# Layer 1's sums of a graph attention kernel: two slot tiles as one product of 64 weight columns per head

## The chip, the cores and the metric

The kernel runs on one core of a Trainium2 chip. The metric is the device time of one execution in microseconds (us); a version is stated by the median of its runs. A core has TensorE (PE, matrix products; its loads of weights are listed apart, as PEld), VectorE (DVE), ScalarE (ACT), GpSimd (POOL) and SyncE (SP, which here issues transfers). TensorE multiplies a stationary operand, the weights, of up to 128 rows by 128 columns with a moving operand that streams through, and adds into PSUM. Sixteen DMA engines move data between the memory (HBM) and the core.

## What is computed

Two graph attention layers over 3125 nodes and 53125 edges (each drawn edge in both directions, and a self loop per node), with edges sorted by destination. Cut to what matters here, layer 1 (4 heads of 256 columns, 1024 in all):

```python
xl = (x @ W).reshape(n, heads, out_ch)
e = leaky_relu(alpha_src[src] + alpha_dst[dst], 0.2)
e = exp(e - segment_max(e, dst)[dst])
alpha = e / (segment_sum(e, dst)[dst] + 1e-16)
out = segment_sum(xl[src] * alpha[:, :, None], dst)
```

The last line is the part that the change touches: for each node and head, the weighted sum of the rows `xl[src]` of its edges. A layer norm, a ReLU and a residual product follow, then layer 2 with one head of 768 columns, built in the same way.

## The kernel before

**Node tiles and slot tiles.** Nodes lie in 25 tiles of 128 (the last has 53). The edges of a node tile are laid out by an earlier stage of the kernel in 17 slot tiles of 128 slots each (8 in the last node tile), so that the edges of each quarter (32 nodes) of the tile fall in known slot tiles. `QUARTERS` (L33) says which quarters a slot tile can hold: the fifth, ninth and thirteenth (numbers 4, 8 and 12) lie across two quarters, 0 and 1, 1 and 2, 2 and 3; each other slot tile belongs to one.

```python
QUARTERS = [(0,), (0,), (0,), (0,), (0, 1), (1,), (1,), (1,), (1, 2), (2,), (2,), (2,), (2, 3), (3,), (3,), (3,), (3,)]
ROUNDS = [(0, 5, 9, 13), (1, 6, 10, 14), (4, 11, 15), (2, 8, 16), (3, 7, 12)]
```

**One slot tile's part of the sum.** POOL gathers the 128 source rows of 1024 numbers from `table1` in HBM into a tile `g` (`gather`, L197 and L201; thirteen such tiles are held, so gathers run about three rounds ahead). DVE makes the weights `w` (`weights_of`, L734 and L735): for each slot a one-hot row over the 32 nodes of its quarter, times the slot's attention weight, per head. For a slot tile across two quarters `w` is 64 nodes wide, made in one piece. TensorE then multiplies `w` of a head (32 columns of weights, 128 slots) by `g`'s 256 columns of that head, into the quarter's 32 PSUM partitions of `pa` (L758).

**Rounds.** `ROUNDS` (L34) orders the slot tiles so that each round has four products per head, one for each quarter: in the third round slot tile 4 gives those of quarters 0 and 1, in the fifth slot tile 12 gives those of quarters 2 and 3, and in the fourth slot tile 8 gives those of 1 and 2. The four products of a head stand next to each other in TensorE's order, each with its own quarter of the array's columns. A full round has 16 products of f32, and each f32 product shows in the trace as two weight loads and two matmuls, so 32 records of each. In the last node tile, of 53 nodes, only quarters 0 and 1 exist, and the two halves of a row (heads 0 and 1, heads 2 and 3) lie in different PSUM partitions (0 to 63 and 64 to 127, `half_at`, L188).

**Order of the work.** In `sums` (L655 on) TensorE, ScalarE and VectorE run in the order in which the program is written out. After the products of a round stand the gathers and weights of the next one (`fetch`), and then `step`, which takes one piece of the work beside: the end of an earlier node tile (`finish`, `end1`: own row, norm, transposes at L1174, layer 2's row products at L1196 through `dense`, L182), and pieces of the residual product `later` (L1124, also through L182), as many as `pace` says per round. These products are 128 columns wide; those of the last node tile are 32 and 21 wide (L186). So TensorE's order in this stage is: a round of L758, a stretch of L182 or L1174, a round of L758, and in rounds whose `pace` is zero sometimes two rounds in a row.

Layer 2 has sums of its own (`summed`, L1377, 384 columns wide) with the same rounds; it does not run through `sums`.

Of the kernel before, what the change touches and what calls it, by code (L numbers as in the profile page):

```python
# [32 lines left out]
QUARTERS = [(0,), (0,), (0,), (0,), (0, 1), (1,), (1,), (1,), (1, 2), (2,), (2,), (2,), (2, 3), (3,), (3,), (3,), (3,)]  # L33
# [35 lines left out]
def in_order(  # L69
# [16 lines left out]
    nc = tc.nc  # L86
# [29 lines left out]
    def rows_of(b):  # L116
        return P if b < NB - 1 else LAST
# [4 lines left out]
    def tiles_of(b):  # L122
        return J if b < NB - 1 else JL
# [64 lines left out]
    def half_at(b, i):  # L188

        o = 64 * i if rows_of(b) <= 64 else 0  # L190
        return slice(o, o + rows_of(b))

    def gather(g, table, b, j, whole):

        c = slice(b * J + j, b * J + j + 1)
        if whole:
            nc.gpsimd.indirect_dma_start(  # L197
                out=g, out_offset=None, in_=table[:, :],
                in_offset=bass.IndirectOffsetOnAxis(ap=idx_s[:, c], axis=0))
        else:  # L200
            nc.gpsimd.indirect_dma_start(  # L201
                out=g, out_offset=None, in_=table[:, :],
                in_offset=bass.IndirectOffsetOnAxis(ap=idx_k[:, c], axis=0),
                bounds_check=N - 1, oob_is_err=False)
# [6 lines left out]
    def load_rows(q, t, src_, b):  # L211

        for o, e in pieces(b):
            q.dma_start(t[o:e], src_[b * P + o:b * P + e, :])
# [440 lines left out]
    def sums(heads, cols, table, al, alo_d, ahead, lag, gp, ap, pp, end, more, pace, first=None, delay=0.0):  # L655

        width = heads * cols  # L660
        f = width // 2
        n = min(cols, f)
        running = []
        due = delay

        def step(k):
            nonlocal due
            next(first or iter(()), None)
            for g in list(running):
                if next(g, running) is running:  # L670
                    running.remove(g)
            due += pace[k]
            while due >= 1.0:
                due -= 1.0
                next(more, None)

        def finish(b, own, pa):
            for _ in range(lag):
                yield

            r = rows_of(b)
            v = gp.tile([P, 2, heads], F32, name="aw", bufs=3)[:r]
            aw, share = v[:, 0], v[:, 1]
            ao = asked.pop(b)[:r]
            nc.vector.tensor_scalar(aw, ao[:, :heads, b], has[:r, 1, b:b + 1], has[:r, 2, b:b + 1],
                                    op0=OP.mult, op1=OP.max)
            nc.vector.scalar_tensor_tensor(share, ao[:, heads:, b], has[:r, 0, b:b + 1], aw, op0=OP.mult, op1=OP.add)
            nc.vector.tensor_scalar(share, share, 1e-16, None, op0=OP.add)
            nc.vector.reciprocal(share, share)
            z = gp.tile([P, width], F32, name="z", bufs=2)[:r]  # L690
            for o in range(0, width, n):
                nc.vector.scalar_tensor_tensor(z[:, o:o + n], own[:r, o:o + n], aw[:r, o // cols:o // cols + 1],
                                               pa[half_at(b, o // f), o // f, o % f:o % f + n],
                                               op0=OP.mult, op1=OP.add)
            yield from end(b, z, share)

        asked = {}

        def ask(b):
            ao = asked[b] = ap.tile([128, 2 * heads, NB], F32, name="ao", bufs=3)  # L700
            nc.gpsimd.indirect_dma_start(
                out=ao.rearrange("p v b -> p (v b)"), out_offset=None, in_=alo_d[:, :],
                in_offset=bass.IndirectOffsetOnAxis(ap=at_last[:, b:b + 1], axis=0))

        turns = count()
        owns = {}

        def fetch(b, k):

            got = {}  # L710
            for j in ROUNDS[k]:
                if j >= tiles_of(b):
                    continue
                turn = next(turns)
                g = gp.tile([128, width], F32, name=f"g{turn % ahead}", bufs=1)
                gather(g, table, b, j, turn < ahead)
                got[j] = g, weights_of(b, j)
                place = PLACE[j]
                if place == 4:
                    own = owns[b] = ap.tile([128, width], F32, name="own", bufs=3)  # L720
                    load_rows(nc.sync, own, table, b)
                if b == 1 and place == 11:
                    ask(0)
                if b and place == (13 if tiles_of(b) == J else 5):
                    ask(b)
            return got

        def weights_of(b, j):

            c = b * J + j  # L730
            lo, hi = 32 * QUARTERS[j][0], 32 * QUARTERS[j][-1] + 32
            w = ap.tile([128, heads, hi - lo], F32, name=f"w{hi - lo}", bufs=9 if hi - lo == 32 else 3)
            oh = ap.tile([128, 68], F32, name="oh", bufs=4)[:, :hi - lo]
            nc.vector.tensor_scalar(oh, iota_f[:, lo:hi], rel_s[:, c:c + 1], None, op0=OP.is_equal)  # L734
            nc.vector.tensor_tensor(w, oh[:, None, :].to_broadcast([128, heads, hi - lo]),  # L735
                                    al[:, POS[j], :, b:b + 1].to_broadcast([128, heads, hi - lo]), OP.mult)
            return w

        with tc.manual_schedule(engines={PE, ACT, DVE}):
            ready = fetch(0, 0)  # L740
            for b in range(NB):
                pa = pp.tile([P, 2, 512], F32, name="pa", bufs=2)
                opened = set()
                last_q = (rows_of(b) - 1) // 32
                for k, js in enumerate(ROUNDS):
                    made = []
                    for j, (g, w) in ready.items():
                        for i, q in enumerate(QUARTERS[j]):
                            if q <= last_q:
                                made.append((q, w[:, :, 32 * i:32 * i + 32], g))  # L750
                    order = list(range(0, width, n))
                    if rows_of(b) <= 64:
                        order = [o + i * f for o in range(0, f, n) for i in range(2)]
                    for o in order:
                        for q, w, g in made:
                            to = (o // f, q)
                            p0 = 32 * q + half_at(b, o // f).start
                            nc.tensor.matmul(pa[p0:p0 + 32, o // f, o % f:o % f + n], w[:, o // cols, :],  # L758
                                             g[:, o:o + n], start=to not in opened, stop=False,
                                             skip_group_check=True)  # L760
                            opened.add(to)
                    if k + 1 < len(ROUNDS):
                        ready = fetch(b, k + 1)
                    elif b + 1 < NB:
                        ready = fetch(b + 1, 0)
                    step(k)
                running.append(finish(b, owns.pop(b), pa))
            k = 0
            while running:
                step(k)  # L770
                k = (k + 1) % len(ROUNDS)


    with tc.tile_pool(name="m1", bufs=1) as mp:
# [8 lines left out]
        with tc.tile_pool(name="h0", bufs=1) as hp, tc.tile_pool(name="pm1", bufs=1, space=PSUM) as pm1, \  # L783
# [238 lines left out]
            with tc.tile_pool(name="pq1", bufs=1, space=PSUM) as pp:  # L1022
                with tc.tile_pool(name="sb1", bufs=1) as sb:
                    n = J * H * NB
# [73 lines left out]
        with tc.tile_pool(name="w2", bufs=1, reuse_waits="tile") as wp, tc.tile_pool(name="e1", bufs=2, reuse_waits="tile") as ep, \  # L1098
                tc.tile_pool(name="a1", bufs=1, reuse_waits="tile") as ap, \
                tc.tile_pool(name="g1", bufs=1, reuse_waits="tile") as gp, tc.tile_pool(name="pg1", bufs=1, space=PSUM) as pp:  # L1100
            loaded, made, whole, gone = {}, {}, set(), set()
# [50 lines left out]
            def end1(b, z, share):  # L1152
# [52 lines left out]
                store_rows(nc.sync, table2, b, row)  # L1205

            sums(H, C1, table1, al1, alo1_d, 13, 3, gp, ap, pp, end1, more, (2.5, 3.8, 0, 0, 0.9), first(), -6.3)


    with tc.tile_pool(name="m2", bufs=1, reuse_waits="tile") as mp, \  # L1210
# [3 lines left out]
        f = C2 // 2  # L1214
# [192 lines left out]
        with tc.manual_schedule(engines={PE, ACT, DVE}):  # L1407
# [6 lines left out]
            made = softmax(0)  # L1414
# [9 lines left out]
            for b in range(NB):  # L1424
                pa = pp.tile([P, 2, 512], F32, name="pa")
                opened = set()
                for k in range(len(ROUNDS)):
# [3 lines left out]
                    if b + 1 < NB:  # L1431
                        if k < 3:
                            values(b + 1, k + 2)
                        if k == 2:
                            made = softmax(b + 1)
# [489 lines left out]
```

## Time and profile before

| | |
|---|---|
| median of 3 runs | 1917.48 us (1916.97 to 1924.33) |
| the profiled execution's own time | 1923.87 us |
| its span (first to last instruction) | 1922.0 us |
| mean granted TensorE clock | 0.96 |
| layer 1's sums, by L758's first and last start | 507.0 to 1228.2 us |
| L758: matmul records, median duration of one | 3912, 379 ns |
| L758: weight loads, median duration of one | 3912, 110 ns |

The profile is of one execution, so its times are added up against its own 1923.87 us, of which 1922.0 us lie between the first and the last instruction. A matmul's duration contains the way through the array; matmuls overlap, so durations of records may not be added. "Busy" counts overlapping records once. In a row of a group stand the line, the engine, the operation, what is written and read, the weights' rows and columns (128\*32 is 128 rows by 32 columns) and the moving operand's, the count, then the busy time and the mean duration of one, then the engine's idle time before such instructions and what ended it. "issue" is idle time that ended with no releaser that the profile shows. The granted clock is the share of its full clock that TensorE got.

### The profile page before, as it was taken

The numbers are of one execution on the slowest core, as the hardware profiler recorded it, in microseconds if no ns is written. First come the engines' busy times: TensorE is split into PE (matmuls) and PEld (weight loads), VectorE is DVE, ScalarE is ACT, GpSimd is POOL, SyncE is SP. The second block draws the span as 40 slices with busy tenths as digits, with TensorE's granted clock in tenths as the row PEclk, the third lists the DMA queues.
The fourth block names the chain that finished last, engine by engine and source line by source line (L and its number), as shares of the span: only waits on it lengthen the run. The fifth ranks groups of instructions, "written<-read, shape, count | busy, mean of one in ns | idle before, by whom it ended". The sixth has DMA issues, their size and how long they took to land. (4 is left out here: it accounts for less than half of the span.)

```text
span 1922.0 us, 31113 instructions
## 1 busy us (share of the span) xinstructions
PE 1759.3 (92%) x11411; PEld 957.8 (50%) x11411; DVE 1000.4 (52%) x2641; ACT 443.7 (23%) x1286; POOL 898.9 (47%) x922
## 2 busy tenths in 40 slices
PE   8999998999879999999998998969888898988895
PEld 5666664666446655555554554434333333333331
DVE  7673434888845566466466556312433443344345
ACT  2122331000211212112111211212322332333233
POOL 2000102000365666566566666156566666666662
PEclk9999999999889999999998999889889999989998
DMA  7824538331598999999899999488888998988984
GB/s 236 281 96 144 135 110 295 115 126 64 203 407 314 367 372 348 356 374 385 329 356 378 349 377 333 156 324 313 302 286 324 329 328 325 327 311 310 328 284 157
DMA packets 173673, 540.78 MB, mean 281 GB/s; under 512 B 33086, under 2 KB 58452, under 8 KB 173384
## 3 DMA queue, kind: packets, MB, share of 16 engines
q0 software_dynamic: 100912, 381.05, 55.2%
q1 hardware_dynamic: 68206, 147.26, 21.9%
q10 hardware_dynamic: 4394, 10.39, 1.4%
q8 instruction: 93, 1.52, 0.3%
q14 instruction: 68, 0.56, 0.1%
HBM read 498.62 MB, written 65.62 MB: 294 GB/s over the span
## 5 line engine op out<-in xcount | busy, mean ns | idle before, releaser
L197 POOL DMA_INDIRECT g<-table,idx_s x406 | 405.2, 998 | 411.7 <-DVE m L635 179.2
L201 POOL DMA_INDIRECT g<-table,hi_s x426 | 437.7, 1027 | 291.7 <-issue 88.8
L758 PE MATMUL pa<-g,w 128*32 128x256 f32 x3912 | 275.9, 395 | 32.6 <-issue 23.9
L1377 PE MATMUL pa<-g,w 128*32 128x384 f32 x1956 | 248.8, 510 | 58.9 <-issue 54.4
L182 PE MATMUL pr<-wr,h 128*128 128x384 f32 x768 | 288.0, 516 | 3.8 <-issue 3.8
L182 PE MATMUL p<-w,h1T 128*128 128x384 f32 (+1 forms) x768 | 278.7, 511 | 2.2 <-DVE h1T L1181 1.6
L758 PEld LDWEIGHTS pa<-g,w 128*32 128x32 f32 x3912 | 131.7, 112 | 166.3 <-issue 78.7
L182 PEld LDWEIGHTS pr<-wr,h 128*128 128x128 f32 x768 | 144.8, 200 | 126.2 <-issue 58.2
L182 PEld LDWEIGHTS p<-w,h1T 128*128 128x128 f32 x768 | 145.1, 197 | 123.9 <-issue 32.5
L735 DVE TENSOR_TENSOR w<-oh,al 128x128 f32<-128x128 f32 (+1 forms) x416 | 132.0, 317 | 130.5 <-PE pa L758 75.0
L1377 PEld LDWEIGHTS pa<-g,w 128*32 128x32 f32 x1956 | 63.7, 111 | 221.4 <-issue 208.4
L1341 DVE CUSTOM_DVE_ANT_0 e<-mix,pen 128x640 f32<-128x640 f32 x25 | 20.6, 825 | 290.4 <-remote 132.3
L863 PE MATMUL pm<-w,h0l 128*128 128x344 f32 (+1 forms) x468 | 140.8, 455 | 0.0
L182 PE MATMUL pr<-h0k,wr 128*128 128x256 f32 (+1 forms) x576 | 140.1, 390 | 0.0
L1000 PE MATMUL pm<-h0g,wr 128*128 128x512 f32 x288 | 132.7, 607 | 0.1
L863 PE MATMUL pm<-w,h0g 128*128 128x344 f32 x432 | 131.0, 459 | 0.3 <-ACT h0g L842 0.3
L182 PEld LDWEIGHTS pr<-h0k,wr 128*128 128x128 f32 x576 | 106.2, 190 | 29.5 <-issue 9.0
L931 POOL DMA_DIRECT2D hot_d<-ohd x25 | 13.4, 538 | 219.5 <-DVE own L513 120.6
L734 DVE TENSOR_SCALAR oh<-iota_f,rel_s 128x32 f32<-128x32 f32 (+1 forms) x416 | 113.4, 272 | 0.1
L863 PEld LDWEIGHTS pm<-w,h0l 128*128 128x128 f32 (+1 forms) x468 | 84.8, 185 | 44.1 <-issue 5.7
L863 PEld LDWEIGHTS pm<-w,h0g 128*128 128x128 f32 x432 | 81.9, 193 | 40.8 <-issue 1.7
L1320 ACT ACTIVATE slots<-g 128x32 f32<-128x32 f32 x416 | 65.1, 219 | 117.8 <-DMA g<-table,idx_s 77.7
(288 smaller groups left out, 1666.8 us busy)
## 6 DMA issues: line engine op xcount, KB each, us to landing
s<-slo_d SPq DMA_DIRECT2D x25, 544.0 KB
table<-row SPq DMA_DIRECT2D x24, 512.0 KB
own<-table SPq DMA_DIRECT2D x24, 512.0 KB
h1T_d<-h1T SPq DMA_DIRECT2D x24, 512.0 KB
h<-h1T_d SPq DMA_DIRECT2D x22, 512.0 KB
table<-row SPq DMA_DIRECT2D x24, 392.0 KB
ring<-in_x_dram SPq DMA_DIRECT2D x24, 384.0 KB
xr<-in_x_dram SPq DMA_DIRECT2D x24, 384.0 KB
```

Source lines behind the costliest of these rows:

```text
L182: nc.tensor.matmul(out_, lhsT, rhs, start=start, stop=stop)
L197: nc.gpsimd.indirect_dma_start(out=g, out_offset=None, in_=table[:, :], in_offset=bass.IndirectOffsetOnAxis(ap=idx_s[:, c], axis=0))
L201: nc.gpsimd.indirect_dma_start(out=g, out_offset=None, in_=table[:, :], in_offset=bass.IndirectOffsetOnAxis(ap=idx_k[:, c], axis=0), bound ...
L734: nc.vector.tensor_scalar(oh, iota_f[:, lo:hi], rel_s[:, c:c + 1], None, op0=OP.is_equal)
L735: nc.vector.tensor_tensor(w, oh[:, None, :].to_broadcast([128, heads, hi - lo]), al[:, POS[j], :, b:b + 1].to_broadcast([128, heads, hi - ...
L758: nc.tensor.matmul(pa[p0:p0 + 32, o // f, o % f:o % f + n], w[:, o // cols, :], g[:, o:o + n], start=to not in opened, stop=False, skip_gr ...
L863: nc.tensor.matmul(pm[:r, :C], h0[b][:, k, :], w1[:, k, i * C:(i + 1) * C], start=(k == 0), stop=(k == NK1 - 1))
L931: nc.gpsimd.dma_start(hot_d[b], ohs[b])
L1000: nc.tensor.matmul(pm, wr1[:, k, m * 128:(m + 1) * 128], groups[gi][:, k, :], start=(k == 0), stop=(k == NK1 - 1))
L1320: nc.scalar.activation(slots[b % 2][:, POS[j], :], gs[b, j][:, C2:C2 + 1].to_broadcast([128, 32]), AF.Copy)
L1341: nc.vector.tensor_tensor_reduce(out=e, in0=mix[:, :WIN], in1=pen, scale=1.0, scalar=-BIG, op0=OP.add, op1=OP.max, accum_out=top)
L1377: nc.tensor.matmul(pa[p0:p0 + 32, i, :f], w_, g[:, i * f:(i + 1) * f], start=(i, q) not in opened, stop=False, skip_group_check=True)
```

## The change

For a slot tile whose first quarter is even (slot tiles 4 and 12, and the slot tiles of quarters 0 and 2 alone), the quarters are taken together: one product per head with all of `w`'s columns, 32 for one quarter and 64 for two, written to 32 or 64 partitions of `pa`. Where the first quarter is odd (slot tile 8, across quarters 1 and 2, and those of quarters 1 and 3) the products stay one per quarter. `last_q` still leaves out quarters that the last node tile does not have.

```diff
                     for j, (g, w) in ready.items():
-                        for i, q in enumerate(QUARTERS[j]):
-                            if q <= last_q:
-                                made.append((q, w[:, :, 32 * i:32 * i + 32], g))
+                        qs = [q for q in QUARTERS[j] if q <= last_q]
+                        if qs[0] % 2:
+                            made += [(q, w[:, :, 32 * i:32 * i + 32], g) for i, q in enumerate(qs)]
+                        else:
+                            made.append((qs[0], w[:, :, :32 * len(qs)], g))
...
-                            nc.tensor.matmul(pa[p0:p0 + 32, o // f, o % f:o % f + n], w[:, o // cols, :],
+                            nc.tensor.matmul(pa[p0:p0 + w.shape[2], o // f, o % f:o % f + n], w[:, o // cols, :],
                                              g[:, o:o + n], start=to not in opened, stop=False,
                                              skip_group_check=True)
```

The third round of a node tile (slot tiles 4, 11, 15) then has three products per head, of 64, 32 and 32 columns in this order; the fifth (3, 7, 12) has three of 32, 32 and 64. The other rounds are as before. The gathers, the weights on DVE and the order of all else stay.

## The prediction

> **What bounds the kernel now.** First the page's busy shares and its costliest groups.
>
> ```profile
> span 1922.0 us, 31113 instructions
> PE 1759.3 (92%) x11411; PEld 957.8 (50%) x11411; DVE 1000.4 (52%) x2641; ACT 443.7 (23%) x1286; POOL 898.9 (47%) x922
> ...
> L758 PE MATMUL pa<-g,w 128*32 128x256 f32 x3912 | 275.9, 395 | 32.6 <-issue 23.9
> ```
>
> TensorE is busy 92% of the span, and the products that the change touches (L758, layer 1's sums) are 275.9 us of it. The reader is to see that 3912 records of 395 ns would be 1545 us one after another, so more than five lie over each other at a time: a product's mean duration, or an average per record, is no price here.
>
> The chain that ended last cannot be used for this stage, for its listing in order of time begins behind the stage, in this row:
>
> ```profile
> 1248.95 6.14 PE p L186 x45
> ```
>
> So I go to the table by stages (us of the stretch; busy time and count of PE, PEld, DVE, ACT, POOL; granted clock; DMA share; GB/s). L758 runs from 507 to 1228 us.
>
> ```profile
> 507.00:700.00 193.00, 176.68 (x1422) 106.73 (x1422) 100.04 (x328) 34.85 (x94) 116.93 (x113) 0.95 0.96 362
> 700.00:900.00 200.00, 197.45 (x1598) 116.14 (x1594) 115.62 (x388) 39.06 (x112) 127.24 (x127) 0.99 0.98 367
> 900.00:1100.00 200.00, 190.76 (x1493) 107.81 (x1491) 115.55 (x383) 33.25 (x94) 124.36 (x124) 0.96 0.96 361
> 1100.00:1228.00 128.00, 122.11 (x926) 66.46 (x927) 71.89 (x234) 23.44 (x69) 71.65 (x76) 0.96 0.88 322
> 507.00:1228.00 721.00, 687.00 (x5430) 397.15 (x5433) 403.10 (x1331) 130.60 (x367) 440.18 (x438) 0.96 0.95 356
> ```
>
> TensorE is busy 687 of 721 us in this stage; DVE and POOL have some 300 us to spare. DMA is close behind, at 0.95. So time added on TensorE moves the end, up to the 34 us in which it now waits; time taken off it would soon meet the transfers.
>
> How four quarters lie beside each other is seen in the timeline of TensorE near the end of the stage (start us, duration us, what, count).
>
> ```profile
> 1209.67 1.93 PE L758 MATMUL pa<-g,w 128*32 128x256 f32 x32
> 1211.53 2.86 PE L182 MATMUL p<-w,h1T 128*128 128x384 f32 x8
> 1214.32 1.07 PE L758 MATMUL pa<-g,w 128*32 128x256 f32 x16
> 1215.32 1.09 PE L1174 MATMUL p<-ident,z 128*128 128x128 f32 x8
> ...
> 1222.45 1.06 PE L758 MATMUL pa<-g,w 128*32 128x256 f32 x8
> 1223.44 4.16 PE L182 MATMUL p<-w,h1T 128*128 128x384 f32 x12
> ```
>
> Each f32 product is two records. A full round (four quarters, four heads, two records: 32) holds TensorE from 1209.67 to 1211.53, 1.86 us. Sixteen records hold it 1.00 us, and the eight of the last node tile's round with one slot tile also hold it 0.99 us. Those eight use only two quarters' columns (the two halves of the row lie in different ones), so both bursts are four steps deep. **The price goes by depth, not by records**: (1.86 - 1.00) / 4 steps gives 0.215 us for one step, in which up to four quarters run side by side, and 1.86 - 8 x 0.215 leaves 0.14 us for going into 32 columns and out again; from the 0.99 it is 0.13.
>
> **The change part by part.** *Fewer products.* In each of 24 node tiles the fifth and the thirteenth slot tile drop from two products to one per head: 24 x 2 x 4 products, and 4 more in the last node tile for its fifth, 196 in all, so 392 matmul records and 392 weight loads go. Of the 3912 records 3128 stay 32 columns wide and 392 become 64 wide. By depth this takes nothing off: in the round of slot tiles 4, 11 and 15, quarters 0 and 1 were already side by side with 2 and 3, two steps per head, and the wide product still needs its two steps. Bounds of this part: zero, and by the average per record 392 x 275.9 / 3912 = 27.6 us gained. I take zero, because the eight-record row is the nearest and lies on it.
>
> *Two widths in one round.* Now the round issues, per head, one 64-column product and two 32-column ones (the wide one first in the round of 4, 11, 15, last in that of 3, 7, 12), so the width changes twice per head. No row of before shows a change between 64 and 32. The nearest are the changes between 128 and smaller, and one stretch 53 columns wide:
>
> ```profile
> 291.94 0.38 PE L545 MATMUL pd<-tabd,ohd 128*128 128x96 bf16 x5
> 292.25 10.61 PE L863 MATMUL pm<-w,h0l 128*53 128x344 f32 x36
> 302.80 0.39 PE L545 MATMUL pd<-tabd,ohd 128*128 128x96 bf16 x5
> ...
> 809.62 1.02 PE L182 MATMUL pr<-h0k,wr 128*128 128x256 f32 x4
> 810.58 1.93 PE L758 MATMUL pa<-g,w 128*32 128x256 f32 x32
> ```
>
> Four 256-column steps at full width take 4 x 0.215 = 0.86 us but hold TensorE 0.96 before 32 columns begin: 0.10 us is lost at the change of width alone, though nothing is waited for. The 53-column stretch holds 10.55 us for 36 steps of 344 columns; a step is 344/256 x 0.215 = 0.289, so 0.15 us goes for its change in and out, as much as for 32 columns. [...]
>
> [...]
>
> If the widths take turns, each head has two segments instead of one: two steps for the wide product, then two for the pair. One segment costs 2 x 0.215 + 0.13 = 0.56 us. A round has 4 heads x 2 = 8 segments, 4.48 us, where it took 1.86: **2.62 us more**. There are 24 x 2 = 48 such rounds (the last node tile's fifth slot tile stands alone in its round, on both halves of the row, so it costs one more change, 0.13 us): 48 x 2.62 = **126 us** on TensorE. Bounds: nothing, if the wide product runs beside the two narrow ones; 83 us, if they take turns but nothing is lost at a change (8 x 0.43 + 0.14 - 1.86 = 1.72 per round); 130 us with 0.15 in place of 0.13 for the wide segments. I take 126, since each change of width in the trace has that loss.
>
> *What gives some back.* TensorE waits 34 us in this stage. The waits view of the stage (who waits for whom: us in total, times, longest), with DVE's wait for TensorE in it:
>
> ```profile
> DVE w L735 <- PE pa L758: 75.0, 32, 6.0
> ...
> PE pa L758 <- issue: 23.9, 37, 1.3
> ...
> PE pa L758 <- DMA g<-table,hi_s: 2.9, 3, 2.1
> ```
>
> A place where such waits lie, in the timeline, and the page's group of the gathers:
>
> ```profile
> 932.70 0.39 PE L758 MATMUL pa<-g,w 128*32 128x256 f32 x1 [0.85 <-issue]
> 934.11 0.42 PE L758 MATMUL pa<-g,w 128*32 128x256 f32 x2 [1.02 <-issue]
> 935.56 1.98 PE L758 MATMUL pa<-g,w 128*32 128x256 f32 x15 [1.02 <-issue]
> ```
> ```profile
> L201 POOL DMA_INDIRECT g<-table,hi_s x426 | 437.7, 1027 | 291.7 <-issue 88.8
> ```
>
> Single products here start 1.41 and 1.45 us apart. A gather keeps POOL about 1 us (1027 ns), so I read these as rounds that stand for gathered rows arriving one by one; the view itself says only that it sees no releaser. Such idling also lowers the granted clock, 0.96 against 0.99 in the stretch from 700 to 900 where little is waited for. With 5.2 us more on TensorE per node tile, the gathers come early instead. From 700 to 1228, 528 - 510.3 = 17.7 us are idle, and the clock shortfall is 0.01 x 200 + 0.04 x 200 + 0.04 x 128 = 15 us: at most 33 can come back, at least nothing. I take 20, most of it, because these short waits end once the rows are ahead; the first 193 us, before the gathers have any lead, I leave as they are. Would emptier columns lower the clock? No:
>
> ```profile
> 292.20:302.80 10.60, 10.60 (x40) 4.53 (x37) 2.00 (x12) 2.08 (x6) 0.53 (x1) 1.00 0.62 204
> ```
>
> 53 busy columns for ten microseconds kept it at 1.00.
>
> *Nothing else moves.* Gathers, weights on DVE and stores are issued in the same order; the wide weights are already made in one piece. DVE already waits 75 us for TensorE to free weight buffers and will wait longer, which costs nothing while DVE is not the bound. Layer 2 has its own products and keeps its time.
>
> **Sum.** 126 - 20 = 106 us. The profiled execution took 1923.9 us (1922.0 us of span and 1.9 around it) and would become 2030; it lies 6.4 above the median of the three runs, 1917.5, which becomes **2023 us**.
>
> **The rivals.** *The wide product runs beside the narrow ones* (chance 0.12). Quarters 0 and 1 belong to one and 2 and 3 to the others throughout the round, so no column changes its owner, whereas every change seen in the trace takes over columns of the product before. Against it: the loss was alike for 32 and 53 columns. Then a round stays two steps per head and the time stays at about 1917 us, no change.
>
> *They take turns but lose nothing in between* (0.07). The loss at a change may come from columns that change hands, and a queue that is one for each width would still separate them. 83 - 15 given back = 68 us: 1986 us.
>
> *Records have a price* (0.03). This one ends faster: 27.6 us less, 1890 us, if the average per record held; it decides from the point where fewer records let the four quarters start closer together. Against it stands the row of eight records, which took as long as sixteen, and a DMA share of 0.95 that would not let the stage shrink as far. [...]
>
> **How the numbers follow.** The forecast, turns with a loss at each change, gets 0.78; the rivals 0.12, 0.07 and 0.03. Its own spread goes from 126 - 43 (the 33 given back, and 10 of the 16 us that the first 193 stand idle) to 130 and some more for longer weight loads ahead of 64 columns: 2000 to 2060. The range must leave out no more than 0.2; without the no-change and the faster rival 0.15 is gone, so it reaches down to the second rival with some room, 1975, and up to 2060. About 0.5%, 9.6 us, is what a measurement of this kernel can tell from no change. Slower 0.78 + 0.07 = 0.85, same 0.12, faster 0.03.
>
> **What would show it.** In the profile of the changed kernel L758 should stand in two forms, 392 records 128*64 and 3128 of 128*32, with some 400 us of busy time together. In the timeline, rounds of 24 records should hold TensorE near 4.5 us and pure rounds of 32 still 1.86; the stage should end near 1335 instead of 1228, with its DMA share down to about 0.83 and fewer waits of L758. If rounds of 24 hold 1.86 us, the first rival is right; at 3.6 the second. It would be wrong in size if the waits of L758 stay at 34 us, or if the clock falls in the mixed rounds.

## The result and the profile after

The changed kernel took 2015.8 us (median of 4 runs, 2013.15 to 2029.32) against 1917.2 us (median of 4) before. The ratio is 1.0517 with a 95% interval of 1.0478 to 1.0555: 98.6 us slower. A later measurement, against its own runs of the kernel before, gave 1.0547 (1.0503 to 1.0591). The forecast was 2023 us. The profiled execution took 2013.15 us.

The page of the changed kernel: span, busy shares, the group of the changed products (now L760), and the queue that will matter below.

```profile
span 2011.2 us, 30329 instructions
PE 1847.1 (92%) x11019; PEld 957.5 (48%) x11019; DVE 998.3 (50%) x2641; ACT 445.9 (22%) x1286; POOL 904.9 (45%) x922
...
q8 instruction: 90, 1.47, 0.3%
...
L760 PE MATMUL pa<-g,w 128*32 128x256 f32 (+1 forms) x3520 | 384.3, 392 | 20.9 <-issue 12.7
```

392 records are gone, and the products' busy time has gone up from 275.9 to 384.3 us all the same. The groups of L760 with its two shapes apart (in the stretch from 500 to 1330 us):

```profile
L760 PE MATMUL pa<-g,w 128*32 128x256 f32 x3128 | 282.2, 390 | 20.6 <-issue 12.5 <-DVE w L735 4.7 <-DMA g<-table,hi_s 3.3
...
L760 PE MATMUL pa<-g,w 128*64 128x256 f32 x392 | 125.8, 406 | 0.4 <-issue 0.2 <-DMA g<-table,hi_s 0.2
```

In the tile view of `pa`, L760 starts at 508.7 and last at 1319.1 us: the stage lasts 810 us instead of 721. What lies ahead of it (507.0 and 508.7 us) and behind its last start (693.8 and 692.1 us, the span less that start) kept its length. All of the loss is in this stage, and there it is in the mixed rounds:

```profile
902.57 4.60 PE L760 MATMUL pa<-g,w 128*32 128x256 f32 x24
907.10 2.86 PE L182 MATMUL p<-w,h1T 128*128 128x384 f32 x8
909.79 1.02 PE L182 MATMUL pr<-h0k,wr 128*128 128x256 f32 x4
910.75 1.93 PE L760 MATMUL pa<-g,w 128*32 128x256 f32 x32
912.61 1.09 PE L1176 MATMUL p<-ident,z 128*128 128x128 f32 x8
```

A mixed round of 24 records holds TensorE from 902.57 to 907.10, 4.53 us; the pure round of 32 records behind it still holds it 1.86 us. The forecast had 4.48 and 1.86. The reader should look at starts of neighbours here, not at the durations: the pure round's row lasts 1.93 us, as its last record of 0.38 us runs on into the next line's first. (A merged row prints the shape of its first record; this one, of the fifth round, begins with 32 columns.)

The stage as a whole, in the columns of the table by stages shown before:

```profile
509.00:1319.00 810.00, 789.88 (x5038) 402.25 (x5040) 402.05 (x1330) 130.48 (x367) 439.67 (x438) 0.99 0.88 317
```

TensorE is now idle 20 us in it instead of 34, at a granted clock of 0.99 instead of 0.96, and the DMA share went from 0.95 to 0.88. So TensorE, busy 790 of 810 us, bounds the stage.

### The profile page after: what moved, and what is told of

Same layout as the page of the kernel before. It is cut to its first block, busy times and chain, and to the rows that moved or that the text cites. A ratio compares the mean times of both kernels' runs of the same rounds, so it can differ in the third digit from the quotient of the medians.

```text
span 2011.2 us, 30329 instructions
## 1 busy us (share of the span) xinstructions
PE 1847.1 (92%) x11019; PEld 957.5 (48%) x11019; DVE 998.3 (50%) x2641; ACT 445.9 (22%) x1286; POOL 904.9 (45%) x922
## 3 DMA queue, kind: packets, MB, share of 16 engines
q8 instruction: 90, 1.47, 0.3%
## 5 line engine op out<-in xcount | busy, mean ns | idle before, releaser
L197 POOL DMA_INDIRECT g<-table,idx_s x406 | 414.6, 1021 | 424.1 <-DVE m L635 179.4
L760 PE MATMUL pa<-g,w 128*32 128x256 f32 (+1 forms) x3520 | 384.3, 392 | 20.9 <-issue 12.7
L1379 PE MATMUL pa<-g,w 128*32 128x384 f32 x1956 | 237.9, 513 | 69.7 <-issue 41.0
L182 PE MATMUL p<-w,h1T 128*128 128x384 f32 (+1 forms) x768 | 273.5, 504 | 1.7 <-DVE h1T L1183 1.6
L760 PEld LDWEIGHTS pa<-g,w 128*32 128x32 f32 (+1 forms) x3520 | 139.3, 113 | 257.4 <-issue 185.4
L1379 PEld LDWEIGHTS pa<-g,w 128*32 128x32 f32 x1956 | 61.8, 111 | 224.3 <-issue 176.2
```

The costliest lines, as they stand in the source:

```text
L182: nc.tensor.matmul(out_, lhsT, rhs, start=start, stop=stop)
L197: nc.gpsimd.indirect_dma_start(out=g, out_offset=None, in_=table[:, :], in_offset=bass.IndirectOffsetOnAxis(ap=idx_s[:, c], axis=0))
L760: nc.tensor.matmul(pa[p0:p0 + w.shape[2], o // f, o % f:o % f + n], w[:, o // cols, :], g[:, o:o + n], start=to not in opened, stop=False, ...
L1379: nc.tensor.matmul(pa[p0:p0 + 32, i, :f], w_, g[:, i * f:(i + 1) * f], start=(i, q) not in opened, stop=False, skip_group_check=True)
```

## The experiments

The first three runs share a chip on which the kernel before takes 1804.7 us; the next four share a second chip (1924.65 us), the last three a third (1921.5 us). Only ratios, and differences within a chip, can be compared with the rest.

**Fewer changes of width in a mixed round.** The first run issues the wide products of all four heads, then the narrow ones (two segments a round); the second does so for heads in pairs (four segments). The changed kernel has eight.

```diff
-                    for o in order:
-                        for q, w, g in made:
+                    widths = sorted({w.shape[2] for _, w, _ in made}, reverse=True)
+                    for o, (q, w, g) in [(o, m) for n_ in widths for o in order for m in made if m[1].shape[2] == n_]:
...
+                    for o, (q, w, g) in [(o, m) for os in (order[:2], order[2:]) for n_ in widths for o in os
+                                         for m in made if m[1].shape[2] == n_]:
```

> The changed kernel with another order inside the two mixed rounds of a node tile: first the 64-column products of all four heads, then the 32-column ones, so that the width changes once in a round instead of seven times. Theory (the two widths take turns, and each change of width loses 0.13 us): a mixed round goes from 4.5 us to 16 x 0.215 + 2 x 0.13 = 3.70 us, which is 48 x 0.83 = 40 us less on TensorE; with what is given back, about 1980 us. Rival (the wide product is itself slow, whatever stands beside it): no difference from the changed kernel, 2016 us, the round at 4.5 us. Rival (only the change costs, the widths could share a step): the round falls to about 2.0 us and the time to 1920.

> As the run before, but the heads in two pairs, so the width changes three times in a mixed round. Theory: 16 x 0.215 + 4 x 0.13 = 3.96 us for a round, halfway in the count of changes, about 1992 us. Rival (the wide product is itself slow): 2016 us. If the loss at a change were not a constant, the round would not lie on the line through 4.5 us (eight segments) and the run before (two).

Measured: 1878.4 us, 1.0415 (1.0392 to 1.0438), with two segments, and 1890.0 us, 1.0472 (1.0448 to 1.0495), with four. TensorE's timeline, first with two segments:

```profile
630.16 3.79 PE L761 MATMUL pa<-g,w 128*64 128x256 f32 x24
633.88 2.86 PE L182 MATMUL p<-w,h1T 128*128 128x384 f32 x8
```

and with four:

```profile
633.08 4.06 PE L762 MATMUL pa<-g,w 128*64 128x256 f32 x24
637.07 2.86 PE L182 MATMUL p<-w,h1T 128*128 128x384 f32 x8
```

The rounds hold TensorE 3.72 and 3.99 us. With 4.53 for eight segments the three lie on a line: 0.27 / 2 and 0.54 / 4 are both 0.135 us for a segment, and what is left at none is 3.45 us, sixteen steps of 0.216. Both halves of the theory are seen apart: the widths take turns (3.45 us, where four narrow quarters need eight steps, 1.73), and each segment loses 0.135 us. The rival that only changes cost (2.0 us a round) and the one of a slow wide product (4.5 us whatever the order) both fall. The times were 73.7 and 85.3 us over before, where 63 and 75 had been expected: the rounds were right, what came back was less, 16 and 17 of 89 and 102 us. In the three traces from this chip these products have no wait at all without a named releaser, where the kernel before had 23.9 us of them in its trace from another chip; it was not traced on this one.

**One of the two places.**

```diff
-                        if qs[0] % 2:
+                        if qs[0] % 2 or j == 12:
```

> The changed kernel with the fifth slot tile alone as a wide product; the thirteenth is two 32-column products again. Theory: 24 mixed rounds instead of 48, 63 us more on TensorE than before; with 20 to 30 given back about 1955 us. Rival (the cost is in one of the two places, the wide product first or last in the round): 1917 or 2016 us.

Measured: 1855.5 us, 1.0291 (1.0266 to 1.0316), 50.8 us over its 1804.7. Each place carries its part; a round with the wide product first holds TensorE as long as one with it last (4.53 us in the rows below; the last-placed one of the changed kernel, shown above, 4.53). Of 24 x 2.67 = 64 us added, 13 came back; some 25 had been expected to.

```profile
645.35 4.60 PE L760 MATMUL pa<-g,w 128*64 128x256 f32 x24
649.88 0.59 PE L182 MATMUL p<-w,h1T 128*128 128x384 f32 x1
```

**Wide products without mixing.** Slot tiles 4 and 12 together fill all four quarters, so they can make a round of their own, two wide products side by side. The regrouped rounds are run with narrow products and with the change.

```diff
+ROUNDS1 = [(0, 5, 9, 13), (1, 6, 10, 14), (4, 12), (2, 8, 15), (3, 7, 11, 16)]
...
-                for k, js in enumerate(ROUNDS):
+                for k, js in enumerate(ROUNDS1):
```

> The kernel before, with layer 1's rounds regrouped so that slot tiles 4 and 12 stand alone in the third round (its four quarters come from two slot tiles), then 2, 8, 15 and 3, 7, 11, 16. All products stay 32 columns wide, and every round still has four products per head, each on its own quarter. Both theories: the time of before within 1% (1900 to 1935 us), as no step is added; only the moments at which gathered rows are wanted move.

> The same regrouped rounds with the change: the third round now holds two 64-column products per head, one on quarters 0 and 1 and one on 2 and 3, and no 32-column product; no round is mixed. The same 392 records fewer as in the changed kernel. Theory (the two widths cannot share a step; the wide product alone costs nothing): the third round stays at 8 steps, about 1.9 us with 16 records, and the time equals that of the regrouped kernel with narrow products within 0.5%. Rival (the wide product is itself slow): 24 rounds cost more, some 1960 us. [...]

Measured against before at 1924.65 us: narrow 1933.5 us, 1.0039 (1.0012 to 1.0066); wide 1917.4 us, 0.9978 (0.9953 to 1.0003). The timeline of the wide one:

```profile
625.11 1.95 PE L761 MATMUL pa<-g,w 128*64 128x256 f32 x16
626.99 4.15 PE L183 MATMUL p<-w,h1T 128*128 128x384 f32 x12
631.07 1.93 PE L761 MATMUL pa<-g,w 128*32 128x256 f32 x32
632.93 4.15 PE L183 MATMUL p<-w,h1T 128*128 128x384 f32 x12
```

Sixteen records of 64 columns hold TensorE 1.88 us, the pure narrow round 1.86. So a wide product costs nothing as such; mixing does (4.53 us). Yet the wide one is about 16 us faster by the medians than the narrow one, more than the 0.5% expected, with rounds that take the same time undisturbed. Waits without a named releaser at these products are 22.6 us in the narrow one's trace and 16.2 in the wide one's. This difference, and the one between what was added and what was measured above, needed another cause than changes of width.

**The same TensorE time without a change of width.** Products with zero weights (the tile `zeros`) behind the third and fifth round, on the kernel before, here with six per quarter; the other run has `range(2)`:

```diff
+                    if k in (2, 4) and b < NB - 1:
+                        for _ in range(6):
+                            for q, w, g in made:
+                                nc.tensor.matmul(pa[32 * q:32 * q + 32, 1, f - n:f], zeros, g[:, width - n:],
+                                                 start=False, stop=False, skip_group_check=True)
```

> The kernel before, with two more 32-column products per quarter, of weights that are zero, behind the third and the fifth round of each of the first 24 node tiles: four more steps of 0.215 us, 0.86 us a round, 41 us of TensorE in all, with no change of width. It adds zeros to the sums, so nothing of the computation changes. Theory (the give-back comes first: waits and clock return up to some 30 us, and only what is beyond them shows): about 1930 us. Rival (a fixed share of what is added returns, a quarter): 1949 us.

> The same with six more products per quarter: twelve steps, 2.58 us a round, 124 us of TensorE in all, as much as the change was reckoned to add, again with no change of width. Theory (the time of the changed kernel is nothing but TensorE time added in these rounds, less what the waits and the clock return): within 1% of the changed kernel, 2000 to 2030 us, with the granted clock in the stage near 0.99. Rival (the changes of width do something more, such as keeping weights from being loaded ahead of the next stretch): clearly less than the changed kernel.

Measured: 1966.9 us, 1.022 (1.0166 to 1.0274) with two products, and 2065.5 us, 1.0754 (1.0701 to 1.0808) with six. Both expectations missed, and on the same side: 42 us (by the interval 32 to 53) for 41 added, 141 us (135 to 156) for some 125 added. By the medians nothing came back, and with six, more was lost. An undisturbed round with six:

```profile
647.98 1.93 PE L760 MATMUL pa<-g,w 128*32 128x256 f32 x32
649.73 2.77 PE L767 MATMUL pa<-g,zeros 128*32 128x256 f32 x48
652.44 2.86 PE L184 MATMUL p<-w,h1T 128*128 128x384 f32 x8
```

takes 4.46 us, 2.60 more than a pure one, as reckoned. A disturbed one shows the rest, in TensorE's timeline and in that of its weight loads:

```profile
1020.76 1.96 PE L760 MATMUL pa<-g,w 128*32 128x256 f32 x28
1023.04 0.38 PE L760 MATMUL pa<-g,w 128*32 128x256 f32 x1 [0.32 <-issue]
1023.76 0.39 PE L760 MATMUL pa<-g,w 128*32 128x256 f32 x1 [0.34 <-issue]
1024.48 0.38 PE L760 MATMUL pa<-g,w 128*32 128x256 f32 x1 [0.32 <-issue]
1025.20 0.40 PE L760 MATMUL pa<-g,w 128*32 128x256 f32 x1 [0.35 <-issue]
1025.90 0.53 PE L767 MATMUL pa<-g,zeros 128*32 128x256 f32 x1 [0.30 <-issue]
```
```profile
1023.75 0.13 PEld L760 LDWEIGHTS pa<-g,w 128*32 128x32 f32 x2 [1.29 <-issue]
1025.19 0.11 PEld L760 LDWEIGHTS pa<-g,w 128*32 128x32 f32 x1 [1.32 <-issue]
1025.21 0.11 PEld L767 LDWEIGHTS pa<-g,zeros 128*32 128x32 f32 x1
```

Late gathers can't do this. 28 of the round's 32 records are through, and the zero products read rows that the round has read before them. Single records start 0.72 us apart, loads of weights 1.44 us apart, and the view names nothing that is waited for. The trace of the kernel before had the same, in the row just ahead of the three that the prediction showed:

```profile
930.41 1.45 PE L758 MATMUL pa<-g,w 128*32 128x256 f32 x14
```

A round goes head by head. The first head's 8 records, which ran in two steps of four quarters here too (four starts from 930.41 to 930.43 us, four from 930.65 to 930.67), already read from every gathered tile and every tile of weights of the round. When the single records began, 14 were through, so the rows had arrived.

This looks like instructions that come too slowly. The page counts them in its DMA queues (packets, MB, share), the kernel before first and then the one with six narrow zero products:

```profile
q8 instruction: 93, 1.52, 0.3%
```
```profile
q8 instruction: 111, 1.82, 0.3%
```

0.30 MB for 4608 more records of matmuls and weight loads is 65 bytes a record, so this queue carries TensorE's instructions. The changed kernel, with 784 records fewer of both kinds together, has 90 packets and 1.47 MB. But the queue's packets do not fall where TensorE stands. Around the rows above, the kept trace has one from 1015.29 to 1016.25 us and the next from 1031.33 to 1032.45, none between. Of the 54 waits without a releaser in this stage (25.8 us), 3 overlap a packet, for 0.7 us together, while a packet was under way 7% of the time. So in nearly all of them TensorE was not waiting for a packet of this queue to land; if instructions came slowly, it was somewhere behind the queue.

Two more kernels put the theory to the test: the same streaming, in fewer records. One has three products per quarter of 512 moving columns; the other three of 128 weight columns for all quarters together.

```diff
+                        for _ in range(3):
+                            for q, w, g in made:
+                                nc.tensor.matmul(pa[32 * q:32 * q + 32, 1, :], zeros, g[:, f:],
...
+                        for q, w, g in made[-3:]:
+                            nc.tensor.matmul(pa[:, 1, :], zeros, g[:, f:],
...
```

> The changed kernel once more, on the chip of the two runs that follow. All theories: 1.05 times the kernel before, as in its first measurement.

> The kernel before with zero products behind the third and fifth rounds again, the same 2.56 us of streaming a round as with six narrow products, but three per quarter of 512 moving columns, so 24 records a round in place of 48. It adds zeros to the sums. Theory A (TensorE stands idle in these rounds because its instructions come too slowly: single records start 0.7 us apart in the middle of a round whose operands are all there): fewer records, less standing; between the two, about 1.06 to 1.07 times before. Theory B (it stands for gathered rows): the same TensorE time is added, so 1.075 as with 48 records.

> The same streaming time again, 2.56 us a round, as three zero products of 128 weight columns and 512 moving columns: 6 records a round in place of 48, and no further change of width where a 128-column stretch follows. It adds zeros to the sums. Theory A (instructions come too slowly): TensorE gets 123 us more work and 20 to 35 us of standing come back, as in the changed kernel, so 1.045 to 1.055 times before, with TensorE idle in the stage below 25 us and half the short stalls gone. Theory B (gathered rows): the same 1.075 as with 48 records, as the transfers get as much more time either way.

Measured against before at 1921.5 us: the changed kernel 2032.0 us, 1.0547 (1.0503 to 1.0591); 24 records 2045.9 us, 1.0669 (1.061 to 1.0728); 6 records 2007.9 us, 1.0447 (1.0413 to 1.0481). An undisturbed round with 24 records, then one with 6:

```profile
644.96 1.93 PE L760 MATMUL pa<-g,w 128*32 128x256 f32 x32
646.72 2.76 PE L767 MATMUL pa<-g,zeros 128*32 128x512 f32 x24
649.40 2.86 PE L184 MATMUL p<-w,h1T 128*128 128x384 f32 x8
```
```profile
657.10 1.93 PE L760 MATMUL pa<-g,w 128*32 128x256 f32 x32
658.97 2.84 PE L766 MATMUL pa<-g,zeros 128*128 128x512 f32 x6
661.64 3.72 PE L184 MATMUL p<-w,h1T 128*128 128x384 f32 x11
```

They hold TensorE 4.44 and 4.54 us. Side by side:

| zero products' records in a round | added on TensorE, 48 rounds | measured over before | chip |
|---|---|---|---|
| 48 | 48 x 2.60 = 125 us | 141 us | second |
| 24 | 48 x 2.58 = 124 us | 124 us | third |
| 6 | 48 x 2.68 = 129 us | 86 us | third |

On one chip the same streaming costs 124 or 86 us, by how it is cut up. The transfers got as much more time in all three, so lateness of the gathers (1.075 for all) falls. The step from 48 to 24 records is not shown: it goes from one chip to another, and the intervals of the two ratios overlap. The step from 24 to 6 is clear of noise, but these products differ also in width and in how many run side by side. So it is shown that the same streaming costs 38 us more as 24 records of 32 columns than as 6 of 128; that the number of records is the cause, or the fetching of instructions behind it, is argued, and no run separates it. With 6 records the waits view of the stage and its row by stages read:

```profile
PE pa L760 <- issue: 8.5, 15, 1.1
...
PE pa L766 <- issue: 0.8, 1, 0.8
```
```profile
507.00:1306.00 799.00, 782.71 (x5723) 437.00 (x5722) 403.29 (x1330) 130.24 (x367) 439.69 (x438) 0.99 0.88 321
```

These products' standing without a named releaser went from 23.9 us before to 9.3, idle time from 34 to 16, and the clock from 0.96 to 0.99, as in the changed kernel. With 48 records "issue" stood at 25.8 us (17.8 at the zero products, 8.0 at the others), with 24 at 13.8, and where single records stand a lone record's 0.38 us, counted as busy, covers half of each gap.

## Why the prediction was right, and where it was not

**What bounds the stage** held: time put on TensorE moved the end of the stage (810 us instead of 721 in the changed kernel), and there what lies outside the stage kept its length.

**Price by depth, not by records** held for the array's own time: 392 fewer records took nothing off a round (1.88 us for 16 wide, 1.86 for 32 narrow). It did not hold for the stage as a whole: zero products cut into 24 narrow records a round cost 38 us more than in 6 wide ones, and the regrouped kernel with 392 records fewer was 16 us faster than its narrow twin. That is the direction of the rival in which records have a price, but not its mechanism, four quarters that start closer together: the undisturbed rounds took the same time. Whether the records or something else about narrow products has that second price is not shown.

**Two widths in one round** held in both parts. The segment was put at 0.56 us, from two steps and the loss at changes between 128 and smaller widths; measured, 4.53 / 8 = 0.566. That 64 and 32 columns take turns was the author's estimate, as no row of before has the two side by side; the runs showed it, with 3.45 us left of a mixed round when its segments' losses are taken off, against 1.73 for eight shared steps. Changes between 64 and 32 columns cost what those between 128 and smaller did: 0.135 us a segment against 0.13 to 0.15 a stretch. The rivals in which the widths share a step, or take turns without loss, would have given 1.86 and 3.6 us a round. The pair of wide products in one round ran side by side (1.88 us for 16 records); the mixed ones did not (4.53 us for 24), though they shared no column. 48 x 2.67 = 128 us were added, against 126 forecast.

**What gives some back** is the step that failed, in its reason. The prediction read the short waits as rounds that "stand for gathered rows arriving one by one", because single products stood 1.4 us apart and a gather keeps POOL about 1 us (1027 ns). That was a likeness of numbers; the view had named no releaser, and the row ahead of those shown had 14 records through, for which every row of the round had to be there. The zero products showed the same gaps where all rows had been read, and with few wide records the gaps shrank. In the changed kernel a mixed round sends 24 records in 4.53 us where 32 went in 1.86, which would fit instructions that keep up, but is not shown to be the cause. The size: 20 us forecast; 128 - 98.6 = 29 us measured by the medians, 17 in the later measurement (110.6 us over before), and 128 - 89 = 39 between the two profiled executions. The profile's own gains are in the same places as forecast: 14 us less idle, and 0.03 more clock, some 24 us of 800. That idle time and clock would return was read from rows; that the 20 us came near, with a reason that does not hold, is luck.

**The adding up** was right within 8 us of the first measurement because the large term, mixed rounds, was right to 2%, for the reason given, and the small one came out at 17 to 29 us.

**Left open.** Why single records come 0.7 us apart in some rounds and not in others was not tried. Two things in the kept traces narrow it. The chip seems to matter: the three traces from the first one have no such wait, though their kernels differ little from the changed one, which has them. The place in the program matters too: counted through L760's 3520 records, single ones stand at numbers 2566 to 2568, 2703 to 2708 and 3423 to 3431 in one trace of the changed kernel and at 2559 to 2562, 2705 to 2708 and 3426 to 3431 in the other. Nor is it settled why the changed kernel (110.6 us on the last chip) gets back less than the kernel with 6-record products (86.4 us) for the same 128 us added; it has fewer records, so their number alone does not order the two. No version was shown faster than before: the regrouped kernel with wide products, 0.9978, has an interval that reaches 1.0003.

## What to carry to other kernels

Before joining narrow products into a wider one, look at what stands beside it: here products of equal width on different columns shared a step (1.88 us for a round's 16 wide records, 1.86 for 32 narrow ones), while products of 64 and 32 columns took turns and lost 0.135 us a segment (4.53 us a round), so join all that share a round or none. Order by width where a mix can't be avoided: with two segments in place of eight the round held TensorE 3.72 us. Idle time without a named releaser is not evidence for the transfer that happens to have a like period: look first at what had already run when the waiting began, then take away the suspected cause before giving it a size.

## What had not been expected of the hardware

In some rounds TensorE got one weight load per 1.44 us, with the round's operands read before, no releaser named and, but for 3 waits of 54, no packet of the instruction queue under way. These waits came at like places of the program in two traces of one kernel, and were absent from the three traces of another chip. What they are stays open. The loss at a change of width was constant, 0.135 us a segment, for two, four and eight segments in a round. Products of 64 and 32 columns share no column, and their changes still cost what those between 128 and 32 did (0.13 to 0.14 us for a pure round).
